# Layer 0's attention on 64x64 tiles of TensorE, with hand-overs between turns of values

## The chip, the cores and the metric

The kernel runs on one core of a Trainium2 chip. The metric is the device time of one execution in microseconds, of the slowest core, here the only one. TensorE (PE) multiplies matrices, VectorE (DVE) reduces and does elementwise work, ScalarE (ACT) computes exponentials and copies, GpSimd (POOL) and SyncE (SP) mainly issue transfers. Each engine works through a queue of its own; where one needs another's result it waits for a semaphore.

## The reference

The input is 8 images of 256 channels and 1024 positions. Layer 0 is an attention with 8 heads of 64, whose softmax runs over the queries (axis 1), not over the keys; layer 1 is an attention over the positions and a mixture of 8 experts with two chosen for each token. Only layer 0's attention is touched:

```
xt = x.reshape(B, C, S).transpose(0, 2, 1)
qkv = (xt @ w_qkv + b_qkv).reshape(B, S, N_HEADS, 3 * D_K)
q, k, v = jnp.split(qkv, 3, axis=-1)
attn = jnp.einsum('bihd,bjhd->bijh', q, k) * SCALE
attn = jax.nn.softmax(attn, axis=1)
res = jnp.einsum('bijh,bjhd->bihd', attn, v).reshape(B, S, N_HEADS * D_K)
res = res @ w_out + b_out + xt
```

All data are float32. A float32 matmul of 512 columns shows in the profile as two recorded passes.

## The kernel before

Images are worked on one after the other. For each one `layer0` runs the attention above, `attend` the first half of layer 1, `normed` the norm ahead of the experts. The routing of an image (`dispatch`, a generator of small VectorE operations and of GpSimd's scatters) is carried along, a portion at a time, in the steps of the next image's `layer0`. The last image takes its own path, and the experts of the other seven run ahead of it.

`layer0` has 32 steps per image: 4 pairs of heads (`g`) times 8 blocks of 128 keys (`j`). One step has, for each of its two heads `h`:

- scores (L390), keys in the partitions of the result and 1024 queries along it, in two banks `n` of 512. A head has 64 channels, so head 0 uses the upper 64 rows of the array and head 1 the lower 64, each with all 128 columns (64x128 tiles). Scores of the two heads are issued next to each other so that the two tiles run together.
- the negated maximum over the queries, in two parts: `first_max` over bank 0 (L401, result `nmax`), and in `soften` over bank 1, combined with the first (L413, writes `scrap`).
- the exponential (L423) over both banks with the sum as a by-product, into `ex`. When it has ended, the buffer of the scores is free.
- after head 1: the reciprocal of both sums (L430), and the values scaled with it (L432, `vs`).

`gather_values` (L448) multiplies the scaled values with the exponentials two steps later (`LAG = 2`), for two heads and two banks, and sums over the 8 key blocks in the two banks of `po`. The stationary operand has 128 keys in the rows and 64 columns, and each head has its half of the columns (128x64 tiles). After the eighth block ScalarE copies `po` to `res`.

The scores have three buffers of two banks (`ps_big`), `po` the last two banks (`ps_acc`). In a step TensorE is given: the scores of head 0, bank 0; those of head 1, bank 1 of the step before; head 0, bank 1; head 1, bank 0; then the values of two steps ago. In 6 of the 32 steps the projection of queries or keys of the next pair of heads follows (L299, full array, evicted by VectorE at L289). What is written here is the program's order; the framework's scheduler sets the final order within each engine from its own estimates, while `issue_after` and `declare_no_dep` add and remove constraints. The engines then run the order that was built.

Of the kernel before, what the change touches and what calls it, by code (L numbers as in the profile page):

```python
# [12 lines left out]
AF = mybir.ActivationFunctionType  # L13
ALU = mybir.AluOpType
AX = mybir.AxisListType


@with_exitstack
def kernel(
# [23 lines left out]
    nc = tc.nc  # L43
    P = 128
# [3 lines left out]
    DK = 64  # L48
    SCALE = DK ** (-0.5)
    NCC = C // P  # L50
    NT = S // P
    NH2 = S // 512
# [21 lines left out]
    def big(name):  # L74

        return ps_big.tile([P, 1024], F32, tag="big", name=name)

    def acc(name):

        return ps_acc.tile([P, 512], F32, tag="acc", name=name)  # L80
# [126 lines left out]
    def bcast(t, n):  # L207

        return t.unsqueeze(2).to_broadcast([P, NT, n])
# [159 lines left out]
    def layer0(b, xT, begun, routing):  # L369

        v, qks = begun.v, begun.qks
        array = None
        res = one.tile([P, NPAIR, S], F32, tag="res", name=f"res_{b}")
        steps = [(g, j) for g in range(NPAIR) for j in range(NT)]
        LAG = 2
        seconds = {}  # L380
        pss, firsts, nmaxes, exps, sums, vss = {}, {}, {}, {}, {}, {}
        po = None

        def score(at, h, n):
            g, j = steps[at]
            q, k = qks[g]
            if n == 0:
                pss[at, h] = big(f"psc_{b}_{g}_{j}_{h}")
            r = slice(h * DK, (h + 1) * DK)
            mm = nc.tensor.matmul(  # L390
                pss[at, h][:, ts(n, 512)], k[r, ts(j, P)], q[r, ts(n, 512)], start=True, stop=True
            )
            if n == 1:

                tc.declare_no_dep(mm.ins, firsts.pop((at, h)).ins, reason="the other bank")

        def first_max(at, h):

            g, j = steps[at]
            nmax = small.tile([P, 1], F32, tag="nmax1", name=f"nmax1_{b}_{g}_{j}_{h}")  # L400
            firsts[at, h] = nc.vector.tensor_reduce(  # L401
                nmax, pss[at, h][:, ts(0, 512)], AX.X, ALU.max, negate=True
            )
            nmaxes[at, h] = nmax

        def soften(at, h):

            g, j = steps[at]
            ps = pss.pop((at, h))
            if h == 0:  # L410
                sums[at] = small.tile([P, 2], F32, tag="sums", name=f"sums_{b}_{g}_{j}")
            nmax = small.tile([P, 1], F32, tag="nmax", name=f"nmax_{b}_{g}_{j}_{h}")
            seconds[h] = nc.vector.tensor_scalar(  # L413
                scrap,
                ps[:, ts(1, 512)],
                -1.0,
                nmaxes.pop((at, h)),
                ALU.mult,
                ALU.min,
                accum_out=nmax,  # L420
            )
            ex = expp.tile([P, 1024], F32, tag="exps", name=f"ex_{b}_{g}_{j}_{h}")
            nc.scalar.activation(  # L423
                ex, ps, AF.Exp, bias=nmax, scale=1.0, accum_out=sums[at][:, h : h + 1]
            )
            exps[at, h] = ex
            if h == 1:

                rs = small.tile([P, 2], F32, tag="rs", name=f"rs_{b}_{g}_{j}")
                nc.vector.reciprocal(rs, sums.pop(at))  # L430
                vs = four.tile([P, 2, DK], F32, tag="vs", name=f"vs_{b}_{g}_{j}")
                nc.vector.tensor_mul(  # L432
                    vs,
                    v[:, j, ts(g, P)].rearrange("p (h d) -> p h d", d=DK),
                    rs.unsqueeze(2).to_broadcast([P, 2, DK]),
                )
                vss[at] = vs

        def gather_values(at):
            nonlocal po  # L440
            g, j = steps[at]
            if j == 0:
                po = [acc(f"po_{b}_{g}_{n}") for n in range(NH2)]
            vs = vss.pop(at)
            exs = [exps.pop((at, h)) for h in range(2)]
            for n in range(NH2):
                for h in range(2):
                    mm = nc.tensor.matmul(  # L448
                        po[n][h * DK : (h + 1) * DK, :],
                        vs[:, h, :],  # L450
                        exs[h][:, ts(n, 512)],
                        start=(j == 0),
                        stop=(j == NT - 1),
                    )
            if j == NT - 1:
                for n in range(NH2):
                    nc.scalar.copy(res[:, g, ts(n, 512)], po[n])
            return mm

        last = len(steps) - 1  # L460
        for at in range(last + LAG + 1):
            if at <= last:
                score(at, 0, 0)
            if 0 < at <= last + 1:
                score(at - 1, 1, 1)
                soften(at - 1, 1)
            if at <= last:

                with tc.issue_after(seconds[1].ins) if 1 in seconds else nullcontext():
                    first_max(at, 0)  # L470
                score(at, 0, 1)
                score(at, 1, 0)
                soften(at, 0)
                with tc.issue_after(seconds[0].ins):
                    first_max(at, 1)
            if at == 0:
                begun.rest()
                next(routing, None)
            if at >= LAG:
                array = gather_values(at - LAG)  # L480
            if at <= last:
                g, j = steps[at]
                if g + 1 < NPAIR and j in (3, 5):
                    if j == 3:
                        qks.append([])
                    qks[g + 1].append(project(b, xT, g + 1, len(qks[g + 1])))
                if array is not None:
                    with tc.issue_after(firsts[at, 1].ins), tc.issue_after(array.ins):
                        next(routing, None)
        for _ in routing:  # L490
            pass


        t1 = one.tile([P, NT, C], F32, tag="t1", name=f"t1_{b}")
        n = 1024 // C
        for i in range(0, NT, n):
            pt = big(f"pt_x_{b}_{i}")
            for j in range(n):
                for cc in range(NCC):
                    nc.tensor.transpose(  # L500
                        pt[:, j * C + cc * P : j * C + (cc + 1) * P], xT[:, cc, ts(i + j, P)], ident
                    )
            nc.vector.tensor_add(
                t1[:, i : i + n, :],
                pt.rearrange("p (j c) -> p j c", c=C),
                b_o.unsqueeze(1).to_broadcast([P, n, C]),
            )
        for i in range(NT):
            pr = acc(f"pr_{b}_{i}")
            for g in range(NPAIR):  # L510
                nc.tensor.matmul(  # L511
                    pr[:, :C], res[:, g, ts(i, P)], wo[:, g, :], start=(g == 0), stop=(g == NPAIR - 1)
                )
            nc.vector.tensor_add(t1[:, i, :], pr[:, :C], t1[:, i, :])
        return t1


    def attend(b, t1, fill, step=nothing):
# [22 lines left out]
        def scores(i):  # L541
# [10 lines left out]
            nmax = small.tile([P, 1], F32, tag="nmax", name=f"nmax_{b}_{i}")  # L552
            nc.vector.tensor_reduce(nmax, psc, AX.X, ALU.max, negate=True)  # L553
            ex = expp.tile([P, 1024], F32, tag="exps", name=f"ex1_{b}_{i}")
# [55 lines left out]
    def gates(b, lT):  # L610


        def tmp(tag):
            return small.tile([P, NT, E], F32, tag=tag, name=f"{tag}_{b}", bufs=1)

        def col(tag):
            return small.tile([P, NT], F32, tag=tag, name=f"{tag}_{b}", bufs=1)
# [12 lines left out]
        m = col("g_m")  # L630
        nc.vector.tensor_reduce(m, l, AX.X, ALU.max)
        p = tmp("g_p")
# [3 lines left out]
        z = col("g_z")  # L636
        nc.vector.tensor_reduce(z, p, AX.X, ALU.add)
        nc.vector.reciprocal(z, z)
# [3 lines left out]
        def first_of_max(src, tag):  # L642
            top, best = col(f"{tag}_top"), col(f"{tag}_best")
            hot = tmp(f"{tag}_hot")
            nc.vector.tensor_reduce(top, src, AX.X, ALU.max)
            nc.vector.tensor_tensor(hot, src, bcast(top, E), ALU.is_equal)
            yield
            nc.vector.tensor_mul(hot, hot, rank)
            nc.vector.tensor_reduce(best, hot, AX.X, ALU.max)
            nc.vector.tensor_tensor(hot, hot, bcast(best, E), ALU.is_equal)  # L650
# [568 lines left out]
```

## Time and profile before

Three runs took 2514.58, 2516.45 and 2519.49 us; the median is 2516.45. The profiled execution has a span of 2513.9 us at a mean granted TensorE clock of 0.995.

| line | engine, what | count | busy us | mean ns of one |
|---|---|---|---|---|
| L390 | TensorE, scores, 64x128 tiles | 2048 passes | 549.4 | 621 |
| L448 | TensorE, values, 128x64 tiles | 2048 passes | 495.9 | 605 |
| L299 | TensorE, projections, full array | 512 passes | 235.0 | 602 |
| L423 | ScalarE, exponential | 512 | 570.6 | 1114 |
| L413 | VectorE, second maximum | 512 | 384.2 | 750 |
| L401 | VectorE, first maximum | 512 | 347.2 | 678 |
| L432 | VectorE, scaled values | 256 | 72.1 | 282 |
| L430 | VectorE, reciprocal | 256 | 40.9 | 160 |

Busy time is the union of a group's spans[...]. That is why 2048 passes of 621 ns fill only 549.4 us: passes overlap, both in the pipeline and as two tiles side by side. Layer 0 takes about 147 us of each image (image 1: from 288 to 435 us). A window of one step, 402.69 to 406.53 us, has TensorE busy for 3.84 us, VectorE for 3.03 and ScalarE for 2.40.

### The profile page before, as it was taken

The page shows a single profiled execution, that of the slowest core. Times are in us where ns is not written, and L with a number is a line of the kernel's source. Part 1 is how long each engine was busy: PE and PEld are TensorE (multiplying, and loading weights), DVE is VectorE, ACT ScalarE, POOL GpSimd, SP SyncE. Part 2 cuts the span into 40 slices and gives each one's busy share as a digit, 9 for nine tenths or more (in the row PEclk, how much of TensorE's full clock was granted, in tenths as well). Part 3 has the DMA queues.
Part 4 walks back from the last instruction along what each step waited for, and adds up shares of the span by engine and source line. Part 5 has one row for each costly group of instructions (what it writes and reads, how often), then busy time and mean ns, then how long its engine had stood idle before and what let it go on. Part 6 is the DMA issues. An engine that isn't in the chain of part 4 may idle for free.

```text
span 2513.9 us, 27737 instructions
## 1 busy us (share of the span) xinstructions
PE 2475.7 (98%) x9919; PEld 1300.1 (52%) x9919; DVE 1547.4 (62%) x3836; ACT 890.6 (35%) x1491; POOL 385.7 (15%) x383
## 2 busy tenths in 40 slices
PE   9999999999999999999999999999999999999799
PEld 3346533653366335633563356434643388886476
DVE  5765677557755775577647764777467753334653
ACT  2551355124512452155314441354135512221222
POOL 0000002000200010001100010001000334444652
PEclk9999999999999999999999999999999999999899
DMA  7992000000000000000000010000000256664353
GB/s 284 385 360 69 34 3 32 17 17 0 28 24 17 1 24 28 9 9 18 34 1 17 13 38 1 17 11 24 1 17 7 74 171 220 213 212 141 125 174 115
DMA packets 82515, 187.62 MB, mean 75 GB/s; under 512 B 13992, under 2 KB 23880, under 8 KB 80584
## 3 DMA queue, kind: packets, MB, share of 16 engines
q1 hardware_dynamic: 57368, 118.65, 13.2%
q0 software_dynamic: 25008, 67.20, 8.5%
q8 instruction: 78, 1.28, 0.2%
q14 instruction: 61, 0.50, 0.1%
HBM read 100.49 MB, written 110.90 MB: 84 GB/s over the span
## 4 chain that ended last, share of the span: by engine, by line
PE 93%; DVE 3%; DMA 2%; ACT 1%; issue 1%; SPq 0%; ACTq 0%; POOL 0%; POOLq 0%; DVEq 0%
PE psc L390 20%; PE po L448 19%; PE pqk L299 9%; PE py L571 9%; PE ps L545 8%; PE pr L511 4%; PE pv L335 4%; PE ph L906 4%; PE pe L931 3%; PE pdy L1113 2%; PE px L530 2%; PE pa L564 2%; PE pdh L1089 2%; PE pt_n L232 1%; PE px L896 1%; DMA wb_x<-wpack,w_at 1%
## 5 line engine op out<-in xcount | busy, mean ns | idle before, releaser
L423 ACT ACTIVATE ex<-psc,nmax 128x1024 f32<-128x1024 f32 x512 | 570.6, 1114 | 556.8 <-DVE scrap L413 492.8
L390 PE MATMUL psc<-qk,qk 64*128 64x512 f32 x2048 | 549.4, 621 | 4.2 <-ACT ex L423 4.0
L448 PE MATMUL po<-ex,vs 128*64 128x512 f32 x2048 | 495.9, 605 | 0.0
L413 DVE TENSOR_SCALAR_CACHE_REDUCE scrap<-psc,nmax 128x512 f32<-128x512 f32 x512 | 384.2, 750 | 160.1 <-PE psc L390 128.0
L390 PEld LDWEIGHTS psc<-qk,qk 64*128 64x128 f32 x2048 | 208.6, 185 | 326.2 <-ACT ex L423 173.4
L401 DVE TENSOR_REDUCE nmax<-psc 128x1 f32<-128x512 f32 x512 | 347.2, 678 | 9.5 <-PE psc L390 9.5
L448 PEld LDWEIGHTS po<-ex,vs 128*64 128x64 f32 x2048 | 124.8, 136 | 335.4 <-issue 211.8
L766 POOL DMA_INDIRECT rows<-n,d_at x112 | 108.9, 972 | 946.5 <-DVE d_at L764 940.0
L571 PE MATMUL py<-n,aT 128*128 128x256 f32 x1024 | 239.9, 388 | 4.8 <-DVE aT L566 4.8
L545 PE MATMUL ps<-nT,xa 128*128 128x512 f32 x512 | 236.5, 592 | 0.0
L299 PE MATMUL pqk<-xT,wqkv 128*128 128x512 f32 x512 | 235.0, 602 | 0.0
L571 PEld LDWEIGHTS py<-n,aT 128*128 128x128 f32 x1024 | 192.8, 192 | 68.6 <-DVE aT L566 43.7
L556 ACT ACTIVATE ex<-ps,nmax 128x1024 f32<-128x1024 f32 x64 | 71.3, 1115 | 341.1 <-DVE nmax L553 334.4
L692 POOL TENSOR_TENSOR t<-t,n 128x2048 f32<-128x2048 f32 x8 | 36.2, 4531 | 905.7 <-issue 629.8
L576 DVE SCALAR_TENSOR_TENSOR t<-py,rs,t 128x256 f32<-128x256 f32 x64 | 31.0, 484 | 215.4 <-PE py L571 215.4
L299 PEld LDWEIGHTS pqk<-xT,wqkv 128*128 128x128 f32 x512 | 93.3, 190 | 132.5 <-issue 93.6
L289 DVE TENSOR_SCALAR qk<-pqk,b_qk 128x512 f32<-128x512 f32 x100 | 75.1, 751 | 110.3 <-PE pqk L299 110.3
L545 PEld LDWEIGHTS ps<-nT,xa 128*128 128x128 f32 x512 | 93.6, 190 | 79.9 <-issue 73.6
L978 POOL DMA_INDIRECT yk<-y,yat x112 | 112.7, 1006 | 92.8 <-DVE o L1010 43.6
L335 PE MATMUL pv<-wqkv,xT 128*128 128x512 f32 x256 | 119.6, 597 | 1.1 <-ACT wqkv L105 1.1
L553 DVE TENSOR_REDUCE nmax<-ps 128x1 f32<-128x1024 f32 x64 | 78.3, 1224 | 59.7 <-PE ps L545 59.7
L511 PE MATMUL pr<-wo,res 128*128 128x256 f32 x512 | 111.8, 379 | 0.0
(191 smaller groups left out, 2439.2 us busy)
## 6 DMA issues: line engine op xcount, KB each, us to landing
rows<-wb SPq DMA_DIRECT2D x7, 8192.0 KB, 51.3
y<-yb SPq DMA_DIRECT2D x63, 256.0 KB, 2.7
xT<-in_x_dram SPq DMA_DIRECT2D x7, 1024.0 KB, 4.9
sums<-t SPq DMA_DIRECT2D x7, 1024.0 KB, 4.4
o<-sums SPq DMA_DIRECT2D x7, 1024.0 KB, 7.7
out_dram<-oT SPq DMA_DIRECT2D x14, 512.0 KB, 5.8
wpack<-in_L_ffn_w_dram SPq DMA_DIRECT2D x4, 1024.0 KB
wb<-in_L_ffn_w_dram SPq DMA_DIRECT2D x16, 256.0 KB, 2.9
```

The costliest lines, as they stand in the source:

```text
L299: mm = nc.tensor.matmul(pq[:, ts(n, 512)], wqkv[:, cc, t, ts(g, P)], xT[:, cc, ts(n, 512)], start=(cc == 0), stop=(cc == NCC - 1),)
L335: nc.tensor.matmul(pv, self.xT[:, cc, ts(i, P)], wqkv[:, cc, 2, :], start=(cc == 0), stop=(cc == NCC - 1),)
L390: mm = nc.tensor.matmul(pss[at, h][:, ts(n, 512)], k[r, ts(j, P)], q[r, ts(n, 512)], start=True, stop=True)
L401: firsts[at, h] = nc.vector.tensor_reduce(nmax, pss[at, h][:, ts(0, 512)], AX.X, ALU.max, negate=True)
L413: seconds[h] = nc.vector.tensor_scalar(scrap, ps[:, ts(1, 512)], -1.0, nmaxes.pop((at, h)), ALU.mult, ALU.min, accum_out=nmax,)
L423: nc.scalar.activation(ex, ps, AF.Exp, bias=nmax, scale=1.0, accum_out=sums[at][:, h : h + 1])
L448: mm = nc.tensor.matmul(po[n][h * DK : (h + 1) * DK, :], vs[:, h, :], exs[h][:, ts(n, 512)], start=(j == 0), stop=(j == NT - 1),)
L511: nc.tensor.matmul(pr[:, :C], res[:, g, ts(i, P)], wo[:, g, :], start=(g == 0), stop=(g == NPAIR - 1))
L545: nc.tensor.matmul(psc[:, ts(n, 512)], xa[:, ec, ts(i, P)], nT[:, ec, ts(n, 512)], start=(ec == 0), stop=(ec == NCC - 1),)
L571: nc.tensor.matmul(py[:, :D], aT[:, ts(m, P)], n1[:, m, :], start=(m == 0), stop=(m == NT - 1))
L766: nc.gpsimd.indirect_dma_start(out=view[:, :], out_offset=bass.IndirectOffsetOnAxis(ap=at, axis=0), in_=n2[:, i, :], in_offset=None,)
L978: nc.gpsimd.indirect_dma_start(out=yk[:, i, k, :], out_offset=None, in_=self.group.y[:, :], in_offset=bass.IndirectOffsetOnAxis(ap=ats[k][ ...
```

## The change

Scores and values of layer 0 are both computed in tiles of 64x64, four of which fill the array. A score matmul is split in two along the keys (columns of the array), and a value matmul in two along the keys (rows of the array, the contraction). The purpose is that the whole of layer 0's attention runs in one tiling of the array.

Splitting a contraction between the upper and lower rows means that two row halves add into the same bank of `po`. [...] So the values of a step come in two turns: in turn 0 the upper half of the keys adds to bank 0 and the lower half to bank 1, in turn 1 the other way round. Turn 0 is issued after the first two score halves of a step, turn 1 after the other two. A half's first matmul in a turn waits until the other half's matmuls of the turn before have ended; an empty instruction on another engine (`relay.nop()`, on GpSimd for image 0, on SyncE later) waits for TensorE there and releases TensorE again.

```
+BEHIND = mybir.DependencyInfo(mybir.DependencyClass.Sync, mybir.DependencyReason.DATA)
...
-        seconds = {}
+        seconds, turned = {}, {}
+
+        relay = nc.gpsimd if b == 0 else nc.sync
...
-            mm = nc.tensor.matmul(
-                pss[at, h][:, ts(n, 512)], k[r, ts(j, P)], q[r, ts(n, 512)], start=True, stop=True
-            )
-            if n == 1:
-
-                tc.declare_no_dep(mm.ins, firsts.pop((at, h)).ins, reason="the other bank")
+            for c in range(2):
+                mm = nc.tensor.matmul(
+                    pss[at, h][ts(c, DK), ts(n, 512)],
+                    k[r, j * P + c * DK : j * P + (c + 1) * DK],
+                    q[r, ts(n, 512)],
+                    start=True,
+                    stop=True,
+                )
+                if n == 1:
+
+                    tc.declare_no_dep(mm.ins, firsts[at, h].ins, reason="the other bank")
...
-        def gather_values(at):
+        def gather_values(at, turn):
...
-            for n in range(NH2):
+            past = dict(turned)
+            for half in range(2):
+                keys = ts(half, DK)
+                n = (half + turn) % 2
                 for h in range(2):
                     mm = nc.tensor.matmul(
-                        po[n][h * DK : (h + 1) * DK, :],
-                        vs[:, h, :],
-                        exs[h][:, ts(n, 512)],
-                        start=(j == 0),
-                        stop=(j == NT - 1),
+                        po[n][ts(h, DK), :],
+                        vss[at][keys, h, :],
+                        exps[at, h][keys, ts(n, 512)],
+                        start=(j == 0 and turn == 0),
+                        stop=(j == NT - 1 and turn == 1),
                     )
+                    if h == 0 and (j > 0 or turn > 0):
+                        tc.add_manual_dep(mm.ins, past[1 - half].ins.name, BEHIND)
+
+                turned[half] = relay.nop()
+                tc.add_manual_dep(turned[half].ins, mm.ins.name, BEHIND)
+            if turn == 0:
+                return mm
...
             if 0 < at <= last + 1:
                 score(at - 1, 1, 1)
                 soften(at - 1, 1)
+            if at >= LAG:
+                gather_values(at - LAG, 0)
...
             if at >= LAG:
-                array = gather_values(at - LAG)
+                array = gather_values(at - LAG, 1)
```

The built program has twice the score and value matmuls, each of half the size, and two hand-overs per turn. The instructions of VectorE and ScalarE are the same in number and kind.

More of the change, by code (lines that the diff above doesn't have):

```diff
@@ L437, in soften @@
                 vss[at] = vs
-        def gather_values(at):
+        def gather_values(at, turn):
             nonlocal po
             g, j = steps[at]
-            if j == 0:
+            if j == 0 and turn == 0:
                 po = [acc(f"po_{b}_{g}_{n}") for n in range(NH2)]
-            vs = vss.pop(at)
-            exs = [exps.pop((at, h)) for h in range(2)]
-            for n in range(NH2):
+            past = dict(turned)
+            for half in range(2):
+                keys = ts(half, DK)
+                n = (half + turn) % 2
                 for h in range(2):
                     mm = nc.tensor.matmul(
-                        po[n][h * DK : (h + 1) * DK, :],
-                        vs[:, h, :],
-                        exs[h][:, ts(n, 512)],
-                        start=(j == 0),
-                        stop=(j == NT - 1),
-                    )
+                        po[n][ts(h, DK), :],
[3 more added lines that the diff above has]
+                        stop=(j == NT - 1 and turn == 1),
+                    )
+                    if h == 0 and (j > 0 or turn > 0):
[4 more added lines that the diff above has]
+                return mm
+            vss.pop(at)
+            for h in range(2):
+                exps.pop((at, h))
             if j == NT - 1:
```

## The prediction

> **What bounds the kernel now.** I read the page's busy shares first, then the chain that ended last, then the timeline of one step of layer 0.
>
> ```profile
> PE 2475.7 (98%) x9919; PEld 1300.1 (52%) x9919; DVE 1547.4 (62%) x3836; ACT 890.6 (35%) x1491; POOL 385.7 (15%) x383
> ...
> PE psc L390 20%; PE po L448 19%; PE pqk L299 9%; PE py L571 9%; PE ps L545 8%; PE pr L511 4%; PE pv L335 4%; PE ph L906 4%; PE pe L931 3%; PE pdy L1113 2%; PE px L530 2%; PE pa L564 2%; PE pdh L1089 2%; PE pt_n L232 1%; PE px L896 1%; DMA wb_x<-wpack,w_at 1%
> ```
>
> TensorE is busy for 98% of the span, and the two groups that the edit touches, scores (L390) and values (L448), are 39% of the chain: about 1000 us in 256 steps. The timeline of one step, image 1 (columns: start us, us, engine, line, operation, tiles, count, idle before):
>
> ```profile
> 402.69 2.04 PE L390 MATMUL psc<-qk,qk 64*128 64x512 f32 x8
> ...
> 403.87 0.75 DVE L413 TENSOR_SCALAR_CACHE_REDUCE scrap<-psc,nmax 128x512 f32<-128x512 f32 x1 [0.69 <-PE psc L390]
> ...
> 404.55 0.68 DVE L401 TENSOR_REDUCE nmax<-psc 128x1 f32<-128x512 f32 x1
> ...
> 404.66 1.94 PE L448 MATMUL po<-ex,vs 128*64 128x512 f32 x8
> 404.73 1.12 ACT L423 ACTIVATE ex<-psc,nmax 128x1024 f32<-128x1024 f32 x1 [1.17 <-DVE scrap L413]
> ...
> 405.35 0.75 DVE L413 TENSOR_SCALAR_CACHE_REDUCE scrap<-psc,nmax 128x512 f32<-128x512 f32 x1
> ...
> 405.74 0.19 ACT L423 ACTIVATION_READ_ACCUMULATOR ex<-psc,nmax 128x1 f32 x1
> ...
> 406.03 0.16 DVE L430 RECIPROCAL rs<-sums 128x2 f32<-128x2 f32 x1
> 406.11 0.67 DVE L401 TENSOR_REDUCE nmax<-psc 128x1 f32<-128x512 f32 x1
> ...
> 406.53 2.06 PE L390 MATMUL psc<-qk,qk 64*128 64x512 f32 x8
> 406.69 0.28 DVE L432 TENSOR_TENSOR vs<-v,rs 128x128 f32<-128x128 f32 x1
> ...
> 407.70 0.75 DVE L413 TENSOR_SCALAR_CACHE_REDUCE scrap<-psc,nmax 128x512 f32<-128x512 f32 x1 [0.67 <-PE psc L390]
> ```
>
> The reader is to see three things. TensorE goes from one step to the next without a pause (402.69 to 406.53 is 3.84). Each half is 8 recorded passes in 4 pairs of concurrent tiles. VectorE waits 0.67 to 0.69 per step for TensorE: TensorE leads, but with under 0.7 us of room. By the starts of L413 an image has 23 plain steps (3.77 to 3.93, mean 3.84), 6 with a projection (7.42 to 7.86, mostly 7.49) and two starting ones (3.0 and 4.7).
>
> [...] pairs start 0.43 apart inside a group (403.23, 403.66), but the last pass of the scores (404.14) and the first of the values (404.66) are 0.52 apart, 0.09 more. [...] After a switch the second pair starts 0.54 after the first for scores (402.69, 403.23) and 0.48 for values (404.66, 405.14): 0.11 and 0.05 too much[...]. [...] the rows above run in their built order. [...]
>
> **The change part by part.**
>
> *Tiles.* 8 full-height or full-width passes per group become 16 of 64x64. The array was full before (two tiles of half of it), so quadrants add no arithmetic rate. What they can remove is the switching between 64x128 and 128x64, twice a step. Four concurrent column tiles are in the trace:
>
> ```profile
> 284.96 0.42 PE L599 MATMUL pl<-n2T,rT 128*32 128x256 f32 x4
> ```
>
> That answer is for 284.96 to 285.1: four tiles have started in it, and the next four come at 285.20 (256 columns, so half of 0.43). I take four quadrants as concurrent at 0.43 a slot. Then TensorE's step is 8 slots, 3.43, a possible gain of 3.84 - 3.43 = 0.41 (0.25 in the scores, 0.16 in the values). The doubled weight loads go beside: 32 per step at the 61 ns of occupied time each that L448's PEld row gives (124.8 / 2048) are 1.95 in 3.43.
>
> *Hand-overs.* Four semaphore instructions per step on GpSimd (image 0) or SyncE (later images); the first value matmul of each half waits for the other half of the turn before. Behind it in TensorE's queue stand the scores of the next turn, for which both maxima wait. Before shows no such relay. Bounds: two hops at 0.10 (the L413 at 403.87, its result read out at 404.63, lets ACT start at 404.73) are 0.20; two at 0.27 (the index cast done at 403.19, GpSimd's L766 at 403.46) are 0.54. With 0.86 for a turn and 0.16 for the drain (a record of 0.59 against its slot of 0.43) that is 1.2 to 1.6 from turn to turn. Score pairs lie between turns, so the spacing is 1.7 at least: hidden, cost 0. I take the lower end; even the upper leaves 0.1. SyncE's loads and stores are built ahead of or behind each image's hand-overs; the store of the sums waits for a GpSimd addition that ends before the first turn.
>
> *VectorE's order.* Splitting the values into turns moves more than the diff shows. In the built order of before, 247 of 256 steps run: L413 head 1, L401 head 0, L413 head 0, reciprocal L430, L401 head 1, values scaled L432. In the changed kernel 238 steps run: second maximum head 1, first maximum head 0, **reciprocal, scaling**, second maximum head 0, first maximum head 1. The reciprocal needs the sums of head 1's exponential, which needs the second maximum just made. So head 0's second maximum stands in a FIFO behind ScalarE's whole exponential, and a circle of one step arises. The end of an image in before shows that path with nothing else on it:
>
> ```profile
> 434.62 0.75 DVE L413 TENSOR_SCALAR_CACHE_REDUCE scrap<-psc,nmax 128x512 f32<-128x512 f32 x1 [0.66 <-PE psc L390]
> ...
> 435.47 1.11 ACT L423 ACTIVATE ex<-psc,nmax 128x1024 f32<-128x1024 f32 x1 [1.20 <-DVE scrap L413]
> ...
> 436.49 0.19 ACT L423 ACTIVATION_READ_ACCUMULATOR ex<-psc,nmax 128x1 f32 x1
> 436.71 0.17 DVE L430 RECIPROCAL rs<-sums 128x2 f32<-128x2 f32 x1 [1.33 <-ACT ex L423]
> 436.91 0.29 DVE L432 TENSOR_TENSOR vs<-v,rs 128x128 f32<-128x128 f32 x1
> ```
>
> Second maximum to reciprocal 2.09; to the scaling 0.20; scaling to the next instruction 0.20 (406.69 to a cast at 406.89); second to first maximum 0.68 (403.87, 404.55); first to the dependent second 0.80 (404.55, 405.35). Sum **3.97 per step**, against 3.84 now and 3.43 for TensorE. VectorE's order takes the place of the drains as the bound. Does TensorE keep up? The latest score pair starts when head 0's exponential frees its buffer, then half a turn, then the pair: by the same durations its result is there about 3.5 after the circle's start, 0.45 early.
>
> *Plain steps:* 8 x 23 x (3.97 - 3.84) = **+24**.
>
> *Projection steps:* TensorE still leads. The projection adds 8 x 0.43 = 3.43, two switches (0.09 + 0.11 and 0.09 + 0.05), less what VectorE's slack gives: I work out 7.23 against 7.48. 8 x 6 x 0.25 = **-12**.
>
> *Routing:* in images 1 to 7 small chained VectorE operations of the image before follow L432 and hide in the 0.7 of waiting. Now they stand between the first maximum of head 1 and its second one, inside the circle. The 0.80 gap hides one (so also the casts of L764); three cost 0.59 (585.65 to 586.23) + 2 x 0.25 (586.43, 586.69, 586.94) + 0.15 - 0.80 = 0.44. By their counts (steps with two, three, three, four, four and five, and some light pairs) 3.6 per image, x 7 = **+25**; from 10 to 30.
>
> *Starts and ends:* the second step of an image loses 0.3, the last two turns have nothing between them and show a hand-over: **about +1**.
>
> Sum: 24 - 12 + 25 + 1 = +38, 2516.45 + 38 = **2555**.
>
> **The rivals.**
> 1. *TensorE stays the bound (faster).* For it: 98% busy, and 0.41 of drains and loads to remove. Against: the built order and the 3.97. It needs the reciprocal not to hold the queue. At 3.55 a step (3.43 and some exposed loads): 184 x 0.29 + 48 x 0.45 = 75 less, **2441**.
> 2. *Quadrants run two at a time.* Then a step is 16 slots, 6.86: 256 x 3.0 more, **3290**. Against: L599's four tiles, and pairs of both kinds already overlapping. No row shows two row and two column tiles together.
> 3. *The hand-over binds.* It needs over 0.95 from the end of a half to the release; with 1.2 the step is 2 x (0.86 + 0.16 + 1.2) = 4.44, +0.47 on the plain and projection steps over my case: 2555 + 232 x 0.47, **2664**. Against: hops of 0.10 to 0.27.
> 4. *Nothing to be measured:* the projections save 0.45 each (22) and routing costs only 2: **2516 to 2520**.
>
> **How the numbers follow.** My case 0.83, rival 1 0.06, rival 2 0.03, rival 3 0.04, rival 4 0.04. Within my case: routing 10 instead of 25 and projections at -0.4 give 24 - 19 + 10 = +15, 2531; 0.07 more at the reciprocal (406.03 is 0.10 after the read-out ended) adds 13, and half a hand-over per image or exposed loads 20 more: 2588. Range 2526 to 2590. Faster by over 0.2% is rival 1 and a little more, 0.07; within 0.2% 0.05; slower 0.88.
>
> **What would show it.** Right: starts of head 1's second maximum 3.95 to 4.05 apart in plain steps; VectorE idle 0.6 to 0.7 before the reciprocal, released by ScalarE's exponential; TensorE busy falling to about 90% in layer 0, with waits for the exponential; score and value slots 0.43 apart with four tiles. Wrong: TensorE without idle time at 3.5 a step (rival 1); slots of two tiles (rival 2); TensorE's waits put down to SyncE or GpSimd (rival 3); reciprocals without a wait, or steps under 3.84.

## The result and the profile after

The changed kernel takes **2619.64 us** (median of 4 runs, 2616.09 to 2624.93) against 2516.47 for the kernel before beside it: ratio 1.0411, 95% interval 1.039 to 1.0431, so 103 us slower. The forecast was slower at 2555, range 2526 to 2590: the direction holds, the size does not. The profiled span is 2623.2 us at a mean granted TensorE clock of 0.982 (before: 0.995).

The page of the kernel after: busy shares, the chain that ended last by engine and by line, and three groups (columns: busy us, mean ns of one; then idle us of the engine just before them and what ended most of it):

```profile
PE 2526.1 (96%) x14015; PEld 1358.5 (52%) x14015; DVE 1570.5 (60%) x3836; ACT 886.7 (34%) x1491; POOL 387.2 (15%) x383
...
PE 62%; DVE 14%; ACT 8%; DMA 2%; issue 2%; ACTq 0%; POOL 0%; SPq 0%; POOLq 0%; DVEq 0%
PE po L460 8%; PE psc L395 8%; PE py L595 8%; PE pqk L300 7%; ACT ex L432 7%; DVE scrap L422 7%; PE ps L569 6%; PE pr L535 4%; PE ph L930 3%; PE pe L955 3%; PE pv L336 3%; PE pdy L1137 2%; DVE nmax L410 2%; PE pdh L1113 2%; PE px L554 2%; PE pa L588 2%
...
L460 PE MATMUL po<-ex,vs 64*64 64x512 f32 x4096 | 719.6, 610 | 50.7 <-ACT res L479 43.0
L395 PE MATMUL psc<-qk,qk 64*64 64x512 f32 x4096 | 726.0, 616 | 11.7 <-ACT ex L432 10.6
...
L439 DVE RECIPROCAL rs<-sums 128x2 f32<-128x2 f32 x256 | 42.4, 166 | 200.1 <-ACT ex L432 200.1
```

Scores and values (now L395 and L460) were 39% of the chain and are 16%; VectorE and ScalarE, which were 4% of it, hold 22%. The reciprocal (L439) waits 200.1 us for ScalarE's exponential: 0.78 for each of the 256. That was expected. Not expected was the 43.0 us in which the values wait for `res`, the copy of `po` (L479).

One plain step, image 1, from the timeline of the kernel after:

```profile
447.57 0.75 DVE L422 TENSOR_SCALAR_CACHE_REDUCE scrap<-psc,nmax 128x512 f32<-128x512 f32 x1
...
448.42 1.11 ACT L432 ACTIVATE ex<-psc,nmax 128x1024 f32<-128x1024 f32 x1 [0.28 <-DVE scrap L422]
...
449.43 0.19 ACT L432 ACTIVATION_READ_ACCUMULATOR ex<-psc,nmax 128x1 f32 x1
449.66 0.17 DVE L439 RECIPROCAL rs<-sums 128x2 f32<-128x2 f32 x1 [0.73 <-ACT ex L432]
...
449.86 0.29 DVE L441 TENSOR_TENSOR vs<-v,rs 128x128 f32<-128x128 f32 x1
450.07 0.74 DVE L422 TENSOR_SCALAR_CACHE_REDUCE scrap<-psc,nmax 128x512 f32<-128x512 f32 x1
...
450.74 0.68 DVE L410 TENSOR_REDUCE nmax<-psc 128x1 f32<-128x512 f32 x1
...
451.55 0.75 DVE L422 TENSOR_SCALAR_CACHE_REDUCE scrap<-psc,nmax 128x512 f32<-128x512 f32 x1
```

From head 1's second maximum to the next one (447.57 to 451.55) is 3.98; to the reciprocal 2.09; from the reciprocal to the scaling 0.20; the next maxima follow at once. VectorE starts nothing in the 0.73 before the reciprocal, and head 0's second maximum (450.07) comes behind the scaling. This is the circle of the prediction, link by link.

The differing place is the step in which the values of a **new pair of heads** begin: three per image, 24 in all. There, turn 0 of key block 0 starts new sums in both banks of `po`, which ScalarE must have copied to `res` before. The timeline of the kernel after:

```profile
436.60 0.75 DVE L422 TENSOR_SCALAR_CACHE_REDUCE scrap<-psc,nmax 128x512 f32<-128x512 f32 x1
...
437.08 1.06 ACT L479 COPY res<-po 128x512 f32<-128x512 f32 x2
...
437.71 1.13 PE L460 MATMUL po<-ex,vs 64*64 64x512 f32 x6 [1.66 <-ACT res L479]
...
440.18 1.07 PE L460 MATMUL po<-ex,vs 64*64 64x512 f32 x2
...
443.59 0.75 DVE L422 TENSOR_SCALAR_CACHE_REDUCE scrap<-psc,nmax 128x512 f32<-128x512 f32 x1 [1.44 <-PE psc L395]
```

and of the kernel before, at the same place:

```profile
410.38 2.04 PE L390 MATMUL psc<-qk,qk 64*128 64x512 f32 x8
...
411.14 1.07 ACT L457 COPY res<-po 128x512 f32<-128x512 f32 x2
...
412.35 1.94 PE L448 MATMUL po<-ex,vs 128*64 128x512 f32 x8
```

Before, the copies run beside a whole score group and end 0.14 before the next values need the banks (411.14 + 1.07 = 412.21). After, only one score pair of 0.86 lies between the last turn into the old sums and turn 0 of the new ones, and the copies stand in ScalarE's queue behind head 0's exponential, which VectorE's order has made late: TensorE stands still for 1.66 us. In the 24 places it is 1.66 to 1.88 us.

Then comes a second cost. The next lines are by windows of the kernel after (columns: stretch, its length, busy us and count of PE, PEld, DVE, ACT and POOL, then the granted clock of TensorE, DMA share, GB/s). First the plain step above, then a microsecond after the pause, then another step with a new pair:

```profile
447.57:451.55 3.98, 3.98 (x38) 1.70 (x34) 3.16 (x10) 2.41 (x5) 0.97 (x1) 1.00 0.09 33
440.00:441.00 1.00, 1.00 (x8) 0.35 (x4) 0.56 (x1) 0.00 (x0) 0.00 (x0) 0.50 0.00 0
899.68:904.97 5.29, 4.19 (x38) 2.00 (x42) 3.10 (x9) 3.85 (x8) 0.00 (x0) 1.00 0.00 0
```

After the pause the clock is 0.50. Slots of four tiles then follow each other by 0.85 instead of 0.43, so the step from 436.60 to 443.59 takes 6.99. The clock record in the trace has it at half from 438.76 on, for 3.41 us. A new-pair step with the pause but at full clock takes 5.29; that of the last line above has its pause here (timeline of the kernel after):

```profile
900.78 1.13 PE L460 MATMUL po<-ex,vs 64*64 64x512 f32 x6 [1.88 <-ACT res L479]
```

In this profile 17 stretches of layer 0 run at half clock, 16 of them after one of the 24 pauses; in that of before none do. The first window also shows why PE's busy time is a poor sign here: 8 slots of 0.43 are 3.43 us of work, yet all 3.98 count as busy, because each record lasts 0.6 and covers the pauses between slots.

### The profile page after: what moved, and what is told of

It reads as the page before. It is cut to its first block, busy times and chain, and to the rows that moved or that the text cites. A ratio compares the mean times of both kernels' runs of the same rounds, so it can differ in the third digit from the quotient of the medians.

```text
span 2623.2 us, 36876 instructions
## 1 busy us (share of the span) xinstructions
PE 2526.1 (96%) x14015; PEld 1358.5 (52%) x14015; DVE 1570.5 (60%) x3836; ACT 886.7 (34%) x1491; POOL 387.2 (15%) x383
## 3 DMA queue, kind: packets, MB, share of 16 engines
q1 hardware_dynamic: 57368, 118.65, 12.6%
## 4 chain that ended last, share of the span: by engine, by line
PE 62%; DVE 14%; ACT 8%; DMA 2%; issue 2%; ACTq 0%; POOL 0%; SPq 0%; POOLq 0%; DVEq 0%
PE po L460 8%; PE psc L395 8%; PE py L595 8%; PE pqk L300 7%; ACT ex L432 7%; DVE scrap L422 7%; PE ps L569 6%; PE pr L535 4%; PE ph L930 3%; PE pe L955 3%; PE pv L336 3%; PE pdy L1137 2%; DVE nmax L410 2%; PE pdh L1113 2%; PE px L554 2%; PE pa L588 2%
## 5 line engine op out<-in xcount | busy, mean ns | idle before, releaser
L460 PE MATMUL po<-ex,vs 64*64 64x512 f32 x4096 | 719.6, 610 | 50.7 <-ACT res L479 43.0
L395 PE MATMUL psc<-qk,qk 64*64 64x512 f32 x4096 | 726.0, 616 | 11.7 <-ACT ex L432 10.6
L395 PEld LDWEIGHTS psc<-qk,qk 64*64 64x64 f32 x4096 | 199.2, 135 | 398.1 <-issue 205.9
L460 PEld LDWEIGHTS po<-ex,vs 64*64 64x64 f32 x4096 | 221.5, 135 | 311.3 <-issue 136.5
L439 DVE RECIPROCAL rs<-sums 128x2 f32<-128x2 f32 x256 | 42.4, 166 | 200.1 <-ACT ex L432 200.1
```

Of the source, the lines that this page charges most:

```text
L395: mm = nc.tensor.matmul(pss[at, h][ts(c, DK), ts(n, 512)], k[r, j * P + c * DK : j * P + (c + 1) * DK], q[r, ts(n, 512)], start=True, stop ...
L460: mm = nc.tensor.matmul(po[n][ts(h, DK), :], vss[at][keys, h, :], exps[at, h][keys, ts(n, 512)], start=(j == 0 and turn == 0), stop=(j == ...
```

## The experiments

The sums below are worked out from the traces: the step lengths between starts of head 1's second maximum, less those of the kernel before at the same step, in us over the whole run. "Plain" are 90 steps; "routing" are 70 in images 1 to 7 at the steps with routing. The last column is the sum of the others; for the changed kernel it makes up the whole 103 us.

| kernel | plain | routing | new pair (24) | projection (48) | starts and between images | layer 0 in all |
|---|---|---|---|---|---|---|
| after | +13.3 | +33.9 | +63.2 | -9.9 | +3.3 | +103.9 |
| after_again | +13.0 | +33.8 | +56.8 | -9.9 | +3.3 | +97.0 |
| e3_fill | +12.6 | +33.8 | +34.2 | -9.9 | +3.3 | +74.0 |
| e2_late | +13.5 | +33.9 | +22.1 | -9.7 | +4.5 | +64.2 |
| e1_order | -24.3 | -8.4 | +27.3 | -4.8 | +0.6 | -9.6 |
| e4_before_order | +43.4 | +31.2 | +11.9 | +23.5 | +11.4 | +121.4 |
| e6_scale_first | -31.8 | -1.8 | +24.6 | -15.5 | +0.2 | -24.3 |
| e7_split | -27.2 | +5.9 | +2.9 | -16.8 | +0.2 | -35.0 |
| e8_late | -31.6 | -1.8 | +12.5 | -13.9 | +4.7 | -30.0 |
| e11_late_but_first | -30.8 | -1.7 | +12.5 | -15.9 | +0.2 | -35.8 |

The theory to be tested: the time goes to VectorE's order (all steps) and to the pause at a new pair with its half clock; quadrants and hand-overs cost nothing. Its rival: the quadrants or the hand-overs themselves are slow, and VectorE only waits with them. The runs were made on three chips of this kind, on which the kernel before takes 2542 to 2550 us; so ratios are compared. The changed kernel again, on one of them:

> The changed kernel as it is, beside the two versions below. Theory A (its loss lies in layer 0, whatever the rest takes): 3.5 to 4.3% slower than before again; its step times in layer 0 are those of its first profile, 3.98 plain, 5.3 or 7.0 at a new pair of heads, as the clock's windows fall.

It took 2647.04 against 2542.57, ratio 1.0411 (1.0386 to 1.0436): the same ratio as first. Its layer-0 steps are those of the first profile, except that 14 and not 16 of the 24 pauses bring the half clock (new pairs +56.8 instead of +63.2). So the longer times there come from outside layer 0, as far as one profile shows; the kernel before has no profile on these chips.

### VectorE's order

**e1_order** takes reciprocal and scaling out of `soften` into a function `scale`, and calls it one step later, behind head 0's second maximum:

```
-            if h == 1:
...
+        def scale(at):
...
+                if at > 0:
+                    with tc.issue_after(seconds[0].ins):
+                        scale(at - 1)
...
```

> The changed kernel, with one thing undone: the reciprocal and the scaling of the values (L439, L441 there) are issued after head 0's second maximum, as in the kernel before. Theory A (VectorE's order bounds the plain steps, and a wait at each new pair of heads does the rest): plain steps fall from 3.98 to 3.45 to 3.6 us, the routing steps from 4.2 to 4.7 to about 3.6, the exponential no longer holds the copies of po back so long, and the steps at a new pair fall from 5.3 to 7.0 to between 4 and 5: 2470 to 2510 us. Theory B (the quadrants or the hand-overs are slow in themselves): plain steps stay above 3.9, 2600 us or more.

2536.21 against 2544.56, ratio 0.9969 (0.996 to 0.9978). With the same quadrants and hand-overs the plain steps fall from 3.98 to between 3.43 and 3.66, and nothing in layer 0 runs at half clock. The rival is out: quadrants and hand-overs don't need 3.98. TensorE's pause at a new pair shrinks too, from 1.66 to 1.88 down to 0.87 to 0.91, so about half of it came from VectorE's order. What is left over in a 3.66 step, from the timeline of e1_order:

```profile
667.43 0.28 DVE L443 TENSOR_TENSOR vs<-v,rs 128x128 f32<-128x128 f32 x1
...
667.77 0.21 PEld L462 LDWEIGHTS po<-ex,vs 64*64 64x64 f32 x8 [0.88 <-DVE vs L443]
```

The scaling was built behind head 1's first maximum, and the weight load of the values now waits for it.

**e6_scale_first** puts that maximum behind the scaling:

```
+                    with tc.issue_after(seconds[0].ins):
+                        scaled = scale(at - 1)
+                with tc.issue_after(scaled.ins if at > 0 else seconds[0].ins):
                     first_max(at, 1)
...
```

> As e1_order, and also the first maximum of head 1 issued behind the scaling of the values (order: second max head 1, first max head 0, second max head 0, reciprocal, scaling, first max head 1). Theory A (with the order mended TensorE's 8 slots of 0.43 are the bound, and the 0.2 above it in e1_order is turn 0 waiting for the values' scaling, which stands behind a first maximum): plain steps fall from 3.66 to 3.43 to 3.5, about 25 us less than e1_order, ratio to before 0.985 to 0.99. Theory B (the 0.2 is the hand-over between turns): plain steps stay at 3.66, ratio 0.997.

2527.74 against 2549.86, ratio 0.9913 (0.9896 to 0.9929). A plain step of e6_scale_first by windows:

```profile
678.00:681.43 3.43, 3.43 (x36) 1.92 (x32) 3.15 (x10) 2.41 (x5) 0.97 (x2) 1.00 0.11 38
```

3.43 is the 8 slots of 0.43: TensorE goes without a pause, four tiles at a time. The 0.41 per step that the prediction put down to the switching between tiles (3.84 - 3.43) is gone; VectorE's order had hidden that. That the 0.41 is made of drains and exposed loads was the author's estimate: no row shows either apart.

**e4_before_order** does the opposite: the kernel before, with 64x128 and 128x64 tiles, is given VectorE's order of after by holding head 0's second maximum behind the last scaling.

```
+            held = h == 0 and "last" in scaled
+            with tc.issue_after(scaled["last"].ins) if held else nullcontext():
+                seconds[h] = nc.vector.tensor_scalar(
...
+                scaled["last"] = nc.vector.tensor_mul(
```

> The kernel before with only VectorE's order of the changed one: head 0's second maximum issued behind the scaling of the values. Tiles, turns and TensorE's order are those of before. Theory A: plain steps go from 3.84 to 3.97, routing steps by another 0.2 to 0.8, projections are unchanged, new pairs of heads show nothing: 2516 + 24 + 24, 2560 to 2568. Theory B (the order costs only together with the quadrants): 2516 to 2522.

2664.02 against 2544.56, ratio 1.047 (1.0452 to 1.0488): 119 us, where about 48 was expected. The order alone, without one quadrant, costs more than the whole change. The expected size was wrong because steps alternate between 3.98 and about 4.72. The timeline of e4_before_order:

```profile
426.20 0.75 DVE L415 TENSOR_SCALAR_CACHE_REDUCE scrap<-psc,nmax 128x512 f32<-128x512 f32 x1
...
427.88 1.94 PE L450 MATMUL po<-ex,vs 128*64 128x512 f32 x8
...
429.75 2.18 PE L390 MATMUL psc<-qk,qk 64*128 64x512 f32 x8
...
430.93 0.75 DVE L415 TENSOR_SCALAR_CACHE_REDUCE scrap<-psc,nmax 128x512 f32<-128x512 f32 x1 [0.81 <-PE psc L390]
```

Here head 1's scores miss their turn: a whole group of values (1.94) has just started, and VectorE waits 0.81 more for scores behind it. In the changed kernel a turn of values of 0.86 lies between score pairs, and the same order costs its plain steps 13.3 us in all, not 43.4. So the change as a whole bears this order better than the kernel before; that the finer interleaving is the reason fits the timeline, but was not tested apart from the tiles.

### The new pair of heads

**e3_fill** leaves VectorE's order as it is and gives TensorE something to do in the pause: head 0's first scores are computed twice more, into the same place, ahead of turn 0.

```
-        def score(at, h, n):
+        def score(at, h, n, again=False):
...
-            if n == 0:
+            if n == 0 and not again:
...
+            if LAG < at <= last and steps[at - LAG][1] == 0:
+                for _ in range(2):
+                    score(at, 0, 0, again=True)
```

> The changed kernel, with head 0's first score half computed three times in place of once in the steps where a new pair of heads begins (21 to 24 times 1.7 us of work in TensorE's wait, same results). Theory A1 (of the lost time at a new pair about half is the clock that is halved for 3.4 us after TensorE's pause): steps of 7.0 become 5.3, the granted clock stays at 1.00, about 25 us less, 2595. Theory A2 (the slots of 0.85 us have another cause): nothing falls, 2620 or up to 40 us more by the added work.

2617.94 against 2544.56, ratio 1.0284 (1.0267 to 1.0301). With more work for TensorE the kernel is faster than the change alone: 1.0411 - 1.0284 of 2544.56 is 32 us. Its windows and, ahead of turn 0, its timeline:

```profile
429.71:435.00 5.29, 5.11 (x44) 2.03 (x44) 3.25 (x10) 3.85 (x8) 1.48 (x2) 1.00 0.08 28
```

```profile
430.81 1.13 PE L460 MATMUL po<-ex,vs 64*64 64x512 f32 x6 [0.18 <-ACT res L479]
```

All 24 new-pair steps take 5.28 or 5.29 at clock 1.00, and TensorE idles 0.18 ahead of turn 0. So the half clock is here a consequence of idling, and it is 29 of the 63 us (63.2 - 34.2; in after_again, with fewer stretches, 22.6). The other 34 are the step of 5.29 at full clock: the circle's 3 us, and the wait for the copies, which the fill does not shorten.

**e2_late** moves turn 0 of a new pair behind the second two score halves, where the values of before stand:

```
+            fresh = at >= LAG and steps[at - LAG][1] == 0
-            if at >= LAG:
+            if at >= LAG and not fresh:
                 gather_values(at - LAG, 0)
...
+            if fresh:
+                gather_values(at - LAG, 0)
                 array = gather_values(at - LAG, 1)
```

> The changed kernel, with turn 0 of the first key block of a pair of heads moved to just ahead of its turn 1, so that two score pairs and not one lie between the last turn into the old po and the first into the new one. Theory A: TensorE's wait for the copies of po to res (1.7 us, 24 times) goes, and with it the half clock; the steps at a new pair fall from 5.3 to 7.0 to about 4.2, plain steps stay at 3.98; about 60 us less, 2560. Theory B (the extra time at these steps comes from the hand-over or the exchange of score buffers): no more than 10 us less.

2608.69, ratio 1.0253 (1.0236 to 1.027): 40 us better than after, where 60 was expected. Plain steps stay at 3.98, no new-pair step runs at half clock (one other stretch, in the last image, does), and TensorE no longer stands still ahead of turn 0. But the new-pair steps come down only to 4.79, since ScalarE's copies are still in front of an exponential: in the first new pair of image 1 they start at 388.04, the exponential at 388.98. The second step of nearly every image gets longer (4.4). So the position of turn 0 makes TensorE's pause, and the copies delay the step even without it.

**e7_split** is e6 with the second copy on VectorE, so that the two copies can run side by side:

```
-                    nc.scalar.copy(res[:, g, ts(n, 512)], po[n])
+                    copy = nc.scalar.copy if n == 0 else nc.vector.tensor_copy
+                    copy(res[:, g, ts(n, 512)], po[n])
```

> As e6_scale_first, and one of the two copies of po to res is made by VectorE in place of ScalarE. Theory A (at a new pair of heads turn 0 waits for two copies in a row, which stand behind an exponential on ScalarE): the steps at a new pair lose 0.4 to 0.9 us of about 5.0, 24 times, 10 to 20 us less than e6_scale_first. Theory B (the wait there is for something else, or VectorE's copy comes as late): within 5 us of e6_scale_first.

2519.51 against 2549.86, ratio 0.9872 (0.9856 to 0.9889). The timeline of e7_split:

```profile
406.26 0.68 DVE L483 COPY res<-po 128x512 f32<-128x512 f32 x1
406.48 0.57 ACT L483 COPY res<-po 128x512 f32<-128x512 f32 x1
...
407.00 1.19 PE L463 MATMUL po<-ex,vs 64*64 64x512 f32 x8 [0.80 <-DVE res L483]
```

The new-pair steps are about 4.0, against 4.89 in e6. VectorE pays part of it back: the step ahead of each is mostly 3.83 to 3.89 instead of 3.4. TensorE's pause hardly shrinks, from 0.87 to 0.91 in e6 to 0.71 to 0.84. So the net gain, some 0.5 for the two steps together, is not the pause; it fits the one copy that ScalarE no longer makes ahead of its next exponential, which was not tested further.

**e8_late** joins e6 and e2's move; **e11_late_but_first** does the same but leaves the first pair of heads of an image where it was (`fresh = at > LAG and ...`), since e2 and e8 showed the second step of each image lengthened, by a turn that has no copy to wait for.

> As e6_scale_first, and turn 0 of a new pair of heads moved to just ahead of its turn 1, as in e2_late. Theory A: the copies are hidden under one more score pair, but the hand-over between the two adjoining turns shows, 0.3 to 0.5 us: the steps at a new pair fall from about 5.0 to 4.2 to 4.6, 10 to 20 us less than e6_scale_first. Theory B: no change, or more, because the hand-over costs as much as the copies.

> As e8_late, without moving turn 0 of the first pair of heads of an image, which has no copies to wait for (in e8_late the second step of most images took 4.2 us against 3.6 in e6_scale_first, and the projection after it 0.2 to 0.3 more). Theory A: 8 times 0.6 to 0.9 us less than e8_late, 5 to 7 us, ratio to before about 0.985. Theory B (those steps were longer for another reason): the same as e8_late, 0.987.

e8 took 2519.89, ratio 0.9871 (0.9854 to 0.9888), with new-pair steps of 4.4. e11 took **2509.93** against 2542.57, ratio **0.9863** (0.9842 to 0.9883). It beats both kernels; from e7 and e8 the intervals don't separate it, but its trace shows the second steps of images, 4.23 to 4.28 in seven images of e8, back at 3.41 to 3.66 as in e6.

### The hand-overs

**e9_hops** is e6 with the hand-over lengthened to two hops, through SyncE and GpSimd both:

```
+                past_it = nc.gpsimd.nop() if b > 0 else nc.sync.nop()
+                tc.add_manual_dep(past_it.ins, mm.ins.name, BEHIND)
                 turned[half] = relay.nop()
-                tc.add_manual_dep(turned[half].ins, mm.ins.name, BEHIND)
+                tc.add_manual_dep(turned[half].ins, past_it.ins.name, BEHIND)
```

> As e6_scale_first, with every hand-over made twice as long: TensorE to one engine's empty instruction, from there to a second engine's, and then back to TensorE (GpSimd and SyncE, in the one order or the other). Theory A (a hand-over lies beside a score pair and is hidden): plain steps unchanged, within 5 us of e6_scale_first. Theory B (hand-overs are on the path): one more hop of 0.1 to 0.3 us per turn, two turns a step, 50 to 150 us more.

2740.07 against 2549.86, ratio 1.0732 (1.0711 to 1.0753): neither expectation has that number. The waits of e9_hops (who waits and for what: us in all, times, longest):

```profile
PEld po L463 <- POOLq L475: 174.4, 34, 163.1
...
PE po L463 <- POOLq L475: 162.2, 1, 162.2
```

One step of image 0 takes 174.87: in that image the added hop is on SyncE, which is busy issuing the 8 MB transfers of zeros (L246; 21.21 us for the one at 44.91, and 21 to 22 each for the last five of seven in the trace of after) and behind them the packing of the weights, and reaches its empty instruction only afterwards, at 211.05. That is most of the 190 us. Elsewhere in image 0, and in the first 17 or so steps of the other images, steps are as long as in e6, so a second hop costs nothing there. In the later steps of images 1 to 7, the very ones in which GpSimd, now part of the chain, issues scatters of 0.97 each, plain steps are 4.03 instead of 3.43. What the added hop costs here is what stands ahead of it in the queue that carries it. The change's own choice (GpSimd in image 0, SyncE later) meets neither. Whether the two row halves could add to one bank at the same time is not shown: no run leaves the hand-overs out of a kernel with quadrants.

## Why the prediction was right and wrong

- *The circle of VectorE: right.* 3.98 measured for 3.97, with the reciprocal's wait of 0.73 just above the forecast 0.6 to 0.7. e1 and e6 show that it is the cause, e4 that it needs no quadrants.
- *Routing: right in sum.* Plain and routing steps (160) were to give 160 x 0.13 + 25 = 46; measured 47.2, of which one odd step in image 1 is 5.9 (9.75 against 3.83). Without it the sum is 41.3, so that it comes so close is in part luck.
- *Projections: right in sum.* -12 forecast, -9.9 measured: five of an image's six steps gain mostly 0.2 to 0.4, the third loses 0.28 in images 1 to 7.
- *Tiles and hand-overs: right.* Four tiles at 0.43 a slot, and 3.43 a step in e6. The hand-over costs 0, which e9 bears out for even two hops where their queues are free.
- *Starts and ends: +1 forecast, +3.3 measured.*
- *The step that failed* is "Plain steps: 8 x 23 x (3.97 - 3.84) = +24". It counts as plain the 24 steps in which a new pair begins. They had 3 of the 24 us, and cost 63.2. Two things went unseen. The circle assumes that TensorE is in time, and I checked that for the scores' buffers only, not for `po`: its copies stand behind the exponential that I had myself found to be late, and the change moves their consumer ahead by one score pair. And a pause was priced as its own length: here it also brought a half clock, 29 us more. With this term the forecast would have been 2555 + 60 = 2615. The copy was in the trace of before, with 0.14 to spare.
- *A sign that did not serve:* TensorE's busy share in layer 0 was to fall to 90%. It stays near 97% (2071.83 of the 2140 us from 10 to 2150, in which other stages are included), since records of 0.6 cover the gaps between slots of 0.43, and half-clock passes count as busy. The idle time ahead of a group and the distance of starts are the better signs.
- *Rival 1*, 2441, asked for too much even of the best order: e11 gains 32.6 us, not 75. Routing still holds VectorE in 70 steps (-1.7 in all), and the new pairs still cost 12.5.

The prediction gives plain steps of before as 3.77 to 3.93; in images 1 to 7 one of them is 4.32. Nothing rests on it.

The odd step of 9.75, in which ScalarE waits 7.73 for TensorE's values, comes from TensorE's order in image 1. In after, no value matmul starts there between the first turn (305.88, eight passes) and 317.91: the second turn was built behind 26 score passes, a projection (312.44) and eight more score passes. In image 2 turns and scores alternate from the start, and the step is 4.16. e9 is the one quadrant kernel whose image 1 alternates too, and its step is 3.75. Why the scheduler built image 1 otherwise is not shown.

## What to carry to other kernels

Compare the built order of every engine, not the diff alone: an edit of TensorE's order moved VectorE's reciprocal in 238 of 256 steps and lost all that the edit had gained, and a constraint or two brought it back. When a consumer is moved ahead, look up what frees each of its buffers and what stands in front of that in the freeing engine's queue; the scarce moments are where an accumulator changes hands, and they are to be counted as steps of their own. Route a hand-over over an engine with nothing long in its queue at that time: in e9 one step behind SyncE's transfers took 174.87.

## What the runs showed of the hardware

- A pause of 1.66 to 1.88 us brought TensorE to half clock in 16 of 24 cases (14 in after_again), mostly for 3.41 us, twice for 6.83. The length of the pause alone does not decide it: that of 1.66 before 437.71 did, that of 1.88 before 900.78 did not.
- What goes with it in the trace of after is where the pause lies. In the clock record every stretch at half clock that ends before the kernel does lasts 3.413 us or a multiple of it, and all of them start on one grid of that length (353.4, 397.8 and 438.8 are 13 and 12 such lengths apart). The pause before 437.71 lies wholly in the cell from 435.35 to 438.76, and the next cell is at half clock. The pause before 900.78 is cut in two by the edge at 899.56, and the clock stays full. Count TensorE as idle where no pass of 512 columns has started in the last 0.43 us (0.21 for 256 columns): from 30 to 2140 us, 17 of the 18 full-clock cells with 1.8 us of idle time or more are followed by half clock, and none of those with less (at most 1.70). Why one of the 18 is not, and why two of the stretches last two cells, is open.
- Filling that pause with useless scores (e3) made the kernel 32 us faster.
- From ScalarE's read-out of the sums to VectorE's start is 0.04 us (449.43 + 0.19 to 449.66), where the prediction's range allowed 0.10.
